# Softmax sums of an attention stage: one add chain on VectorE, or two chains on VectorE and GpSimd

## The chip, the cores and the metric

The kernel runs on one core of a Trainium2 chip, in one launch. The metric is the time on the device in microseconds, the median of several runs. A profile of one execution shows when each instruction ran on each engine: PE is TensorE (PEld its weight loads), DVE is VectorE, ACT is ScalarE, POOL is GpSimd, SP is the engine that issues most transfers.

## The reference

The network has four layers over an input of two images with 128 channels and 56 x 56 points. Each layer adds something to its input: attention, a 3x3 convolution, a mixture of experts on 2x2 patches, and a pair of Mamba scans. Only the attention layer matters here. Cut to its core:

```python
qkv = jnp.einsum('oc,bchw->bohw', w_qkv, x).reshape(B, 3, heads, hd, N)   # 4 heads of 32, N = 3136
agent = x.reshape(B, C, a, H // a, a, W // a).mean(axis=(3, 5))           # 49 averages of x
q_to_agent = softmax(einsum('bhnd,bhad->bhna', q * scale, agent))
q_compressed = einsum('bhna,bhad->bhnd', q_to_agent, agent)
attn = softmax(einsum('bhnd,bhmd->bhnm', q_compressed * scale, k))
out = einsum('bhnm,bhmd->bhnd', attn, v)
out = einsum('bnc,oc->bno', out, w_proj) + b_proj
out = layer_norm(out)
```

The large part is `attn` and `out`: for every one of 3136 queries, 3136 exponentials in each head, their weighted average of the values, and their sum, by which the average is divided.

## The kernel before

The layer is the function `short_attention` (L384 on). It works without subtracting a maximum in the softmax. Queries go in blocks of 448 (`BLK`), 7 to an image, 14 in all. Keys go in tiles of 128, 25 to an image, the last of 64. One block is a loop over 25 steps (`STEPS`), a tile of keys each.

A step `i` of a block does this. `score(i)` (L573): TensorE multiplies the tile's keys with the block's queries, head by head, into a PSUM tile `sc`; ScalarE takes the exponential (L586) into `ex`, an SBUF tile of 128 x 4 x 448 fp32, of which there are five in turn. VectorE then adds `ex` to a running sum `ex_sum` (L590 the first of a group, L592 the others). `average` (L594), one step later, multiplies the values with `ex` on TensorE and gathers the product in the PSUM tile `av` over the 25 steps. When it is complete ScalarE copies it to `att`.

The sums that the softmax divides by are still spread over the 128 partitions of `ex_sum`, one per key in a tile. `sum_up` (L615) adds them over partitions with a product of ones: `full`, a matrix of ones, times `ex_sum`, for the four heads, into the PSUM tile `den`. In the kernel before, five tiles make one group (`SUM = 5`), so a block has five `ex_sum` and five products, four in its own loop and the last at step 2 of the next block.

The rest of a block's work is spread over the steps of the next block by a table, `after`: `divide` (L628: `rec` is the reciprocal of `den`, `att` is multiplied by it, and two reductions keep its extremes), `project` (L636: TensorE multiplies `att` with the output weights, ScalarE copies the result to `y`), `measure` (L645: bias and statistics on VectorE), `normalize` (L654: the root by a logarithm and an exponential on ScalarE, with VectorE before and after; then the scaling of `y`), `turn_back` (L667: transposes on TensorE, gain and bias on ScalarE into `z`, and `x + z` on GpSimd, L676) and `restat` (statistics for the next layer). A second table, `ahead`, spreads the preparation of the following block's queries: `q_scores`, `q_softmax` (L543: sums and reciprocal on VectorE, and the multiplication of `a_e` on GpSimd, L548), `q_turn`, `q_mix`. What an image needs at its start (normalization, keys, values) is in a list `rest`, of which a step takes one item where it has no other stage; the second image's items run in the first two blocks.

The order on TensorE, ScalarE and VectorE is written out by hand: each engine takes its instructions in the order in which the loop emits them. A stage that reads a PSUM tile returns a function, `fetch`, which is called at the start of the next step. So an instruction that waits holds up all that is behind it on its engine. Within a step, the add of `score` comes ahead of the stage from `after` or `ahead`. In the attention layer GpSimd has only L548 and L676 once in each block, apart from a few fills.

Of the kernel before, what the change touches and what calls it, by code (L numbers as in the profile page):

```python
# [8 lines left out]
F32 = mybir.dt.float32  # L9
# [8 lines left out]
P = 128  # L18
# [3 lines left out]
BLK = 448  # L22
# [361 lines left out]
def short_attention(net, wide, conv):  # L384
# [12 lines left out]
    tc, nc, a = net.tc, net.nc, net.a  # L397
    heads, hd, agents, side = 4, 32, 49, 7
# [1 line left out]
    na = heads * agents  # L400
    tiles = [(m, min(P, N - m)) for m in range(0, N, P)]
    STEPS = len(tiles)
    SUM = 5
    with ExitStack() as ctx:
        one = ctx.enter_context(tc.tile_pool(name="l0_one", bufs=1))
        work = ctx.enter_context(tc.tile_pool(name="l0_work", bufs=2))
        ps = ctx.enter_context(tc.tile_pool(name="l0_ps", bufs=3, space=PSUM))
# [26 lines left out]
        full = one.tile([P, P], F32, name="full")  # L434
# [88 lines left out]
        class Block:  # L523
# [49 lines left out]
            def score(self, i):  # L573
                at, size = tiles[i]
                if i == 0:
                    self.ex, self.total = {}, {}
                ex = work.tile([P, heads, BLK], F32, name="ex", tag="ex", bufs=5)
                self.ex[i] = ex
                for g in range(2):
                    sc = ps.tile([P, 2, 512], F32, name="sc", tag="sc")  # L580
                    for j in range(2):
                        rows = slice((2 * g + j) * hd, (2 * g + j + 1) * hd)
                        nc.tensor.matmul(  # L583
                            sc[:size, j, :BLK], self.m.k[rows, at : at + size], self.q[rows, :], start=True, stop=True
                        )
                    nc.scalar.activation(ex[:size, 2 * g : 2 * g + 2, :], sc[:size, :, :BLK], AF.Exp, scale=scale)  # L586
                g, n = divmod(i, SUM)
                if n == 1:
                    self.total[g] = work.tile([P, heads, BLK], F32, name="ex_sum", tag="ex_sum")
                    nc.vector.tensor_add(self.total[g], self.ex[i - 1], ex)  # L590
                elif n > 1:
                    nc.vector.tensor_add(self.total[g][:size], self.total[g][:size], ex[:size])  # L592

            def average(self, i):  # L594
                at, size = tiles[i]
# [16 lines left out]

                    return fetch

            def sum_up(self, g):  # L615
                if g == 0:
                    self.den = ps.tile([P, 512], F32, name="den", tag="den", bufs=1)
                for h in range(heads):
                    rows = slice(h * hd, (h + 1) * hd)
                    nc.tensor.matmul(  # L620
                        self.den[rows, :BLK],
                        full[:, rows],
                        self.total[g][:, h, :],
                        start=g == 0,
                        stop=g == STEPS // SUM - 1,
                    )

            def divide(self):  # L628
                rec = work.tile([P, BLK], F32, name="rec", tag="rec")
                nc.vector.reciprocal(rec, self.den[:, :BLK])  # L630
                nc.vector.tensor_mul(self.att, self.att, rec)
                nc.vector.tensor_reduce(ends[:, 0, self.m.b, self.k : self.k + 1], rec, AX.X, ALU.max)
                nc.vector.tensor_reduce(ends[:, 1, self.m.b, self.k : self.k + 1], rec, AX.X, ALU.min)
# [33 lines left out]
            def turn_back(self):  # L667
                z_ps = bank("z_ps")
                for t in range(NT):
                    nc.tensor.transpose(z_ps[:, t * T : (t + 1) * T], self.y[:, t, :], net.ident[:T, :T])  # L670

                def fetch():
                    z = work.tile([P, BLK], F32, name="z", tag="z")
                    nc.scalar.activation(z, z_ps[:, :BLK], AF.Identity, bias=ln_b, scale=ln_g)
                    x = net.xb(self.m.b, self.k)
                    nc.gpsimd.tensor_add(x, x, z)  # L676

                return fetch
# [26 lines left out]
        def values_of(m):  # L705
# [2 lines left out]

        after = {
            4: "divide",  # L710
            6: "project",
            8: "measure",
            10: "normalize",
            13: "turn_back",
            16: "restat",
        }
        ahead = {9: "q_scores", 11: "q_softmax", 15: "q_turn", 18: "q_mix"}
        rest = values_of(images[0])[5:] + taps + opening(images[1])
# [1 line left out]
        with tc.manual_schedule(engines={E.PE, E.Activation, E.DVE}):  # L720
            nc.scalar.preload_act_table_set(EXP_LN)
            late = None
            for stage in opening(images[0]):
                fetch = stage()
                if late:
                    late()
                late = fetch
            late()
            fetches, waiting = [], []
            prev = None  # L730
            for n, blk in enumerate(blocks):
                if n == len(blocks) - 2:
                    pad = one.tile([P, PAD * PAD], F32, name="pad0", tag="xn0")
                    rest = [lambda: conv.norm(0, banks, "mm")]
                    rest += [lambda k=k: conv.pad(0, pad, k) for k in range(NBLK)]
                for i in range(STEPS):
                    for f in fetches:
                        f()
                    fetches = []
                    blk.score(i)  # L740
                    waiting.append((blk, i))
                    quota = 0 if i == 1 else 2 if i == 3 else 1
                    if n == 0 and i == 0:
                        quota = 0
                    for _ in range(quota):
                        if len(waiting) > 1:
                            who, at = waiting.pop(0)
                            fetches.append(who.average(at))
                    if i == 2 and prev:
                        prev.sum_up(STEPS // SUM - 1)  # L750
                    if i >= SUM + 2 and (i - 2) % SUM == 0:
                        blk.sum_up((i - 2) // SUM - 1)
                    stage = None
                    if i in after and prev:
                        stage = getattr(prev, after[i])
                    elif i in ahead and n + 1 < len(blocks):
                        stage = getattr(blocks[n + 1], ahead[i])
                    elif rest and (i > 2 or n == 0):
                        stage = rest.pop(0)
                    if stage:  # L760
                        fetches.append(stage())
                    fetches = [f for f in fetches if f]
                prev = blk
            assert not rest
            while waiting:
                who, at = waiting.pop(0)
                fetches.append(who.average(at))
            prev.sum_up(STEPS // SUM - 1)
            for f in fetches:
                if f:  # L770
                    f()
            tail = [getattr(prev, after[i]) for i in sorted(after)]
            tail[4:4] = [None]
            for k in range(NBLK):
                if k < len(tail) and tail[k]:
                    fetch = tail[k]()
                conv.block(0, k, pad, bank("conv_ps"))
                if k < len(tail) and tail[k] and fetch:
                    fetch()


            bad = net.small.tile([P, 4], F32, name="bad", tag="bad")
            nc.vector.memset(bad, 0.0)
            worst = net.small.tile([P, 4], F32, name="worst", tag="worst")
            aflat = asum.rearrange("t b k h -> t (b k h)")
            for n, (v, op, cmp, limit) in enumerate(
                (
                    (ends[:, 0].rearrange("p b k -> p (b k)"), ALU.max, ALU.is_gt, 1e20),
                    (ends[:, 1].rearrange("p b k -> p (b k)"), ALU.min, ALU.is_lt, 1e-30),
                    (aflat, ALU.max, ALU.is_gt, 1e30),  # L790
                    (aflat, ALU.min, ALU.is_lt, 1e-20),
                )
            ):
                size = v.shape[0]
                nc.vector.tensor_reduce(worst[:size, n : n + 1], v, AX.X, op)
                nc.vector.tensor_single_scalar(bad[:size, n : n + 1], worst[:size, n : n + 1], limit, cmp)
            total = net.small.tile([P, 1], F32, name="bad_sum", tag="bad_sum")
            nc.vector.tensor_reduce(total, bad, AX.X, ALU.add)
            w_ps = bank("w_ps")
            nc.tensor.matmul(w_ps[0:1, 0:1], full[:, 0:1], total, start=True, stop=True)  # L800
            nc.vector.tensor_single_scalar(wide, w_ps[0:1, 0:1], 0.5, ALU.is_gt)
# [1121 lines left out]
```

## Time and profile before

The time before is 3321.07 us (median of 3 runs, 3318.82 to 3325.81). The profiled execution has a span of 3329.8 us.

| | PE | DVE | ACT | POOL |
|---|---|---|---|---|
| busy, whole span | 2938.9 us (88%) | 2182.6 us (66%) | 1699.1 us (51%) | 1466.8 us (44%) |
| busy from 40 to 953 us (attention) | 861.1 us | 723.6 us | 665.1 us | 74.4 us |

The span begins with the loads and the first image's preparation. The attention blocks run from about 40 to 953 us, then come convolution, experts and the Mamba layer. GpSimd's busy time in the first row is nearly all in the Mamba layer.

A line for a group of instructions in the profile gives source line, engine, operation, the tiles written and read with their shapes, and the count; then the time in which the group kept its engine busy and the mean of one in ns; then the time its engine stood idle just before them, and whom it waited for. A line of windows gives a stretch, its length, the busy time of each engine with the number of instructions, and at the end the clock granted to TensorE as a share of full speed, the share of time in which the transfers were busy, and GB/s. A line of waits gives who waited for whom: total us, number of times, longest. A matrix product in fp32 shows as two instructions.

### The profile page before, as it was taken

The page shows a single profiled execution, that of the slowest core. Times are in us where ns is not written, and L with a number is a line of the kernel's source. Part 1 is how long each engine was busy: PE and PEld are TensorE (multiplying, and loading weights), DVE is VectorE, ACT ScalarE, POOL GpSimd, SP SyncE. Part 2 cuts the span into 40 slices and gives each one's busy share as a digit, 9 for nine tenths or more (in the row PEclk, how much of TensorE's full clock was granted, in tenths as well). Part 3 has the DMA queues.
Part 4 walks back from the last instruction along what each step waited for, and adds up shares of the span by engine and source line. Part 5 has one row for each costly group of instructions (what it writes and reads, how often), then busy time and mean ns, then how long its engine had stood idle before and what let it go on. Part 6 is the DMA issues. An engine that isn't in the chain of part 4 may idle for free. (4 is left out here: it accounts for less than half of the span.)

```text
span 3329.8 us, 34063 instructions
## 1 busy us (share of the span) xinstructions
PE 2938.9 (88%) x12828; PEld 1137.2 (34%) x12828; DVE 2182.6 (66%) x1893; ACT 1699.1 (51%) x2504; POOL 1466.8 (44%) x854
## 2 busy tenths in 40 slices
PE   6999999999999799999986788888888888888885
PEld 3333333333334444444443222333323333233321
DVE  5777887887864211111113588888988889888896
ACT  5677777777630111111101466666666665666653
POOL 2000010010000000000003689989999888898896
PEclk9999999999998799999997788988888888888986
DMA  1000000000001687787753544343543435434350
GB/s 50 1 1 1 1 1 1 1 1 1 1 18 37 242 325 291 292 321 300 289 226 109 104 97 88 64 96 79 107 84 71 93 73 107 85 70 93 74 105 7
DMA packets 133396, 333.61 MB, mean 100 GB/s; under 512 B 20101, under 2 KB 90597, under 8 KB 129621
## 3 DMA queue, kind: packets, MB, share of 16 engines
q1 hardware_dynamic: 111616, 304.87, 32.0%
q0 software_dynamic: 5136, 14.70, 1.3%
q10 hardware_dynamic: 16452, 11.61, 1.1%
q8 instruction: 104, 1.70, 0.2%
q14 instruction: 88, 0.71, 0.1%
HBM read 262.56 MB, written 17.20 MB: 84 GB/s over the span
## 5 line engine op out<-in xcount | busy, mean ns | idle before, releaser
L1658 POOL TENSOR_TENSOR dBu<-dtu,Bs 128x896 f32<-128x896 f32 x448 | 947.6, 2139 | 80.0 <-DVE h L1680 66.2
L1680 DVE TENSOR_TENSOR_SCAN h<-dA,dBu 128x896 f32<-128x896 f32 x448 | 887.8, 2010 | 144.1 <-ACT dA L1647 83.7
L586 ACT ACTIVATE ex<-sc 128x896 f32<-128x896 f32 (+1 forms) x700 | 601.4, 918 | 148.0 <-PE sc L583 134.9
L1700 PE MATMUL y<-h,both 128*64 128x448 f32 x1792 | 482.7, 638 | 44.9 <-POOL h L1686 42.3
L592 DVE TENSOR_TENSOR ex_sum<-ex_sum,ex 128x1792 f32<-128x1792 f32 (+1 forms) x210 | 446.1, 2124 | 93.7 <-ACT ex L586 85.1
L583 PE MATMUL sc<-q,k 32*128 32x448 f32 (+1 forms) x2800 | 417.4, 597 | 4.7 <-ACT ex L586 4.1
L1197 PE MATMUL h_ps<-w,xs_c 128*128 128x512 f32 x896 | 392.1, 595 | 10.4 <-issue 9.9
L1647 ACT ACTIVATE dA<-dt,f_A 128x448 f32<-128x448 f32 x448 | 284.2, 636 | 193.2 <-DVE h L1680 163.4
L548 POOL TENSOR_TENSOR a_e<-a_e,a_inv 112x784 f32<-112x784 f32 x14 | 41.6, 2974 | 728.8 <-DVE a_inv L547 728.8
L600 PE MATMUL av<-ex,va 128*32 128x448 f32 (+1 forms) x2800 | 339.5, 560 | 0.0
L1689 DVE TENSOR_TENSOR h<-h,c_ps 128x1792 f32<-128x1792 f32 x154 | 311.3, 2021 | 42.9 <-PE c_ps L1666 28.6
L1647 ACT ACTIVATE dA<-dt,b_A 128x448 f32<-128x448 f32 x448 | 281.5, 635 | 77.9 <-DVE h L1680 69.7
L1201 DVE TENSOR_TENSOR he<-h_ps,sg 128x512 f32<-128x512 f32 x56 | 38.6, 691 | 396.8 <-PE h_ps L1197 373.7
L1148 POOL DMA_INDIRECT xr<-xd,whom x28 | 28.0, 1000 | 600.0 <-PE xr_ps L1187 488.8
L1666 PE MATMUL c_ps<-low,sel_c 40*128 40x448 f32 x308 | 188.2, 696 | 114.9 <-DVE h L1689 73.7
L1686 POOL TENSOR_TENSOR h<-h,Cs 128x1792 f32<-128x1792 f32 x70 | 279.1, 3987 | 19.4 <-issue 18.4
L1197 PEld LDWEIGHTS h_ps<-w,xs_c 128*128 128x128 f32 x896 | 168.5, 190 | 218.4 <-issue 201.9
L1700 PEld LDWEIGHTS y<-h,both 128*64 128x64 f32 x1792 | 121.2, 153 | 356.3 <-issue 273.2
L583 PEld LDWEIGHTS sc<-q,k 32*128 32x128 f32 (+1 forms) x2800 | 142.0, 183 | 239.6 <-issue 128.0
L1218 PE MATMUL o_ps<-w,ht 128*128 128x512 f32 x448 | 200.2, 600 | 7.7 <-DMA w<-in_L_conv_w_dram 7.7
L590 DVE TENSOR_TENSOR ex_sum<-ex 128x1792 f32<-128x1792 f32 x70 | 141.5, 2022 | 89.0 <-ACT ex L586 88.9
L1220 ACT ACTIVATE ot<-o_ps,share 128x512 f32<-128x512 f32 x28 | 19.3, 688 | 286.9 <-PE o_ps L1218 286.9
(322 smaller groups left out, 2972.6 us busy)
## 6 DMA issues: line engine op xcount, KB each, us to landing
w<-in_L_conv_w_dram SPq DMA_DIRECT2D x28, 4096.0 KB, 19.3
w<-in_L_conv_w_dram SPq DMA_DIRECT2D x28, 2048.0 KB, 10.1
Bs<-far SPq DMA_DIRECT2D x56, 896.0 KB, 10.5
dtu<-sp_u SPq DMA_DIRECT2D x112, 224.0 KB, 3.7
dt<-dt SPq DMA_DIRECT2D x112, 224.0 KB, 5.2
Cs<-far SPq DMA_DIRECT2D x140, 112.0 KB, 7.4
os<-ot ACTq DMA_DIRECT2D x28, 256.0 KB, 7.5
xd<-xt SPq DMA_DIRECT2D x14, 224.0 KB, 2.7
```

The lines of the kernel that those rows point to most:

```text
L583: nc.tensor.matmul(sc[:size, j, :BLK], self.m.k[rows, at : at + size], self.q[rows, :], start=True, stop=True)
L586: nc.scalar.activation(ex[:size, 2 * g : 2 * g + 2, :], sc[:size, :, :BLK], AF.Exp, scale=scale)
L592: nc.vector.tensor_add(self.total[g][:size], self.total[g][:size], ex[:size])
L600: nc.tensor.matmul(self.av[rows, :BLK], self.m.va[:size, i, rows], self.ex[i][:size, h, :], start=i == 0, stop=i == STEPS - 1,)
L1197: nc.tensor.matmul(h_ps, xc[:, q, :], w1[:, q, f0 : f0 + 512], start=q == 0, stop=q == 3)
L1218: nc.tensor.matmul(o_ps, ht[:, i, :], w2[:, i, :], start=i == 0, stop=i == nj - 1)
L1647: nc.scalar.activation(self.dA[u][:, r * BLK : (r + 1) * BLK], self.dt2[:, m, r, :], AF.Exp, scale=self.w.A[:, j, 2 * m + r : 2 * m + r + 1],)
L1658: nc.gpsimd.tensor_tensor(self.dBu[u], self.dtu2[:, m], self.B[:, j, :].unsqueeze(1).to_broadcast(shape), ALU.mult)
L1680: nc.vector.tensor_tensor_scan(hf, af, bf, 0.0, ALU.mult, ALU.add)
L1686: nc.gpsimd.tensor_tensor(h4, h4, c, ALU.mult)
L1689: nc.vector.tensor_tensor(h4, h4, c, ALU.mult)
L1700: nc.tensor.matmul(self.y[r * H : (r + 1) * H, m, :BLK], both, self.hc[j][:, m, r, :], start=False, stop=j == PAIRS - 1)
```

## The change

The adding of exponentials is split. Eight of the 25 tiles of a block (`FAR`) are added up by GpSimd in a tile `ex_far`, by seven adds; VectorE adds up the other 17 in one `ex_sum`. After its add of step 19 (`JOIN`) VectorE adds `ex_far` to its sum. A block then needs one product of ones, at step 2 of the next block, where there were five. The change is meant to take the four other products from TensorE and part of the adding from VectorE, and to give `att` more time to be ready: `project` is at step 7 where it was at 6, and the stages after it move along. Two small tiles, `rec` and `z`, have one buffer where they had two, which makes room for `ex_far`.

```diff
-    SUM = 5
+    FAR, JOIN = (0, 1, 3, 5, 7, 9, 13, 15), 19
...
-                g, n = divmod(i, SUM)
-                if n == 1:
-                    self.total[g] = work.tile([P, heads, BLK], F32, name="ex_sum", tag="ex_sum")
-                    nc.vector.tensor_add(self.total[g], self.ex[i - 1], ex)
-                elif n > 1:
-                    nc.vector.tensor_add(self.total[g][:size], self.total[g][:size], ex[:size])
+                if i in FAR:
+                    if i == FAR[1]:
+                        self.far = work.tile([P, heads, BLK], F32, name="ex_far", tag="ex_far", bufs=1)
+                        nc.gpsimd.tensor_add(self.far, self.ex[FAR[0]], ex)
+                    elif i != FAR[0]:
+                        nc.gpsimd.tensor_add(self.far, self.far, ex)
+                else:
+                    near = [n for n in range(i) if n not in FAR]
+                    if len(near) == 1:
+                        self.total = work.tile([P, heads, BLK], F32, name="ex_sum", tag="ex_sum")
+                        nc.vector.tensor_add(self.total, self.ex[near[0]], ex)
+                    elif near:
+                        nc.vector.tensor_add(self.total[:size], self.total[:size], ex[:size])
+                if i == JOIN:
+                    nc.vector.tensor_add(self.total, self.total, self.far)
...
-            def sum_up(self, g):
-                if g == 0:
-                    self.den = ps.tile([P, 512], F32, name="den", tag="den", bufs=1)
+            def sum_up(self):
+                self.den = ps.tile([P, 512], F32, name="den", tag="den", bufs=1)
                 for h in range(heads):
                     rows = slice(h * hd, (h + 1) * hd)
                     nc.tensor.matmul(
-                        self.den[rows, :BLK],
-                        full[:, rows],
-                        self.total[g][:, h, :],
-                        start=g == 0,
-                        stop=g == STEPS // SUM - 1,
+                        self.den[rows, :BLK], full[:, rows], self.total[:, h, :], start=True, stop=True
                     )
...
-                rec = work.tile([P, BLK], F32, name="rec", tag="rec")
+                rec = work.tile([P, BLK], F32, name="rec", tag="rec", bufs=1)
...
-                    z = work.tile([P, BLK], F32, name="z", tag="z")
+                    z = work.tile([P, BLK], F32, name="z", tag="z", bufs=1)
...
             4: "divide",
-            6: "project",
-            8: "measure",
-            10: "normalize",
-            13: "turn_back",
-            16: "restat",
+            7: "project",
+            10: "measure",
+            12: "normalize",
+            14: "turn_back",
+            17: "restat",
...
                     if i == 2 and prev:
-                        prev.sum_up(STEPS // SUM - 1)
-                    if i >= SUM + 2 and (i - 2) % SUM == 0:
-                        blk.sum_up((i - 2) // SUM - 1)
+                        prev.sum_up()
```

## The prediction

> **What bounds the kernel now.** I read the sums of the attention stage first, then its groups of instructions, then the waits, then the order in time of a few microseconds. The stage runs from 40 to 953 us.
>
> ```profile
> 40.00:953.00 913.00, 861.09 (x6659) 285.92 (x6655) 723.57 (x640) 665.10 (x829) 74.35 (x42) 0.97 0.00 1
> L583 PE MATMUL sc<-q,k 32*128 32x448 f32 (+1 forms) x2796 | 417.0, 597 | 4.1 <-ACT ex L586 4.1
> L600 PE MATMUL av<-ex,va 128*32 128x448 f32 (+1 forms) x2800 | 339.5, 560 | 0.0
> L620 PE MATMUL den<-ex_sum,full 128*32 128x448 f32 x552 | 66.4, 554 | 0.0
> L592 DVE TENSOR_TENSOR ex_sum<-ex_sum,ex 128x1792 f32<-128x1792 f32 x196 | 417.9, 2132 | 91.6 <-ACT ex L586 84.3 <-DVE ex_sum L590 0.5
> L590 DVE TENSOR_TENSOR ex_sum<-ex 128x1792 f32<-128x1792 f32 x70 | 141.5, 2022 | 89.0 <-ACT ex L586 88.9
> ...
> PE y_ps L639 <- DVE att L631: 32.0, 13, 2.7
> ACT ir_t L69 <- DVE ir_v L68: 19.2, 15, 6.9
> ```
>
> The first line is the stage by engine in the order PE, PEld, DVE, ACT, POOL: TensorE is busy 861 of 913 us, VectorE 724, ScalarE 665, GpSimd 74. TensorE sets the pace. VectorE's two groups of sums stand idle some 180 us in all, nearly always for ScalarE's exponentials, so VectorE follows with slack. The largest idle time of TensorE is the projection, 32.0 us, for `att`. The copies `att<-av` (L611) start between 119.1 and 953.5 us, 14 of them, so a block takes 834.4 / 13 = 64.2 us. The first block, with the second image's preparation in it, takes about 80.
>
> ```profile
> 339.00:341.00 2.00, 2.00 (x13) 0.50 0.00 0
> 343.00:345.00 2.00, 2.00 (x21) 0.94 0.00 0
> 345.00:347.00 2.00, 2.00 (x20) 1.00 0.00 0
> ```
>
> After the projection's wait (TensorE idle until 337.1 us) the granted clock, the third figure from the right, is 0.50 until about 343 us. So that gap of 2.7 us costs another 3 us of slow products.
>
> The lines that decide my forecast are about GpSimd and VectorE together:
>
> ```profile
> L548 POOL TENSOR_TENSOR a_e<-a_e,a_inv x14: 1501/3087/3090, 33.3 to 862.8; 112x784 f32<-112x784 f32 x14
> L676 POOL TENSOR_TENSOR x<-x,z x14: 1132/2916/2925, 157.2 to 992.0; 128x448 f32<-128x448 f32 x14
> L1686 POOL TENSOR_TENSOR h<-h,Cs x70: 3963/3986/4008, 1873.4 to 3286.0; 128x1792 f32<-128x1792 f32 x70
> ...
> 357.72 3.09 POOL L548 TENSOR_TENSOR a_e<-a_e,a_inv 112x784 f32<-112x784 f32 x1 [59.03 <-DVE a_inv L547]
> 360.77 2.92 POOL L676 TENSOR_TENSOR x<-x,z 128x448 f32<-128x448 f32 x1
> ...
> 357.50 1.96 DVE L592 TENSOR_TENSOR ex_sum<-ex_sum,ex 128x1792 f32<-128x1792 f32 x1
> 359.56 3.13 DVE L592 TENSOR_TENSOR ex_sum<-ex_sum,ex 128x1792 f32<-128x1792 f32 x1
> 362.79 2.78 DVE L592 TENSOR_TENSOR ex_sum<-ex_sum,ex 128x1792 f32<-128x1792 f32 x1
> ```
>
> The first three give shortest, middle and longest duration in ns; the rest are single instructions, start and duration in us. L548 takes 1.50 us once and 3.09 mostly. Put the five in order: VectorE's add ends at 359.46; L548, issued at 357.72, ends at 360.81, 1.35 us after that; VectorE's second add, issued at 359.56, ends at 362.69, 1.88 after L548; L676 ends at 363.69, 1.00 later; the third add ends at 365.57, 1.88 later. They run strictly one after the other, in turn, and the wait is inside the recorded duration.
>
> **What the Trainium skill says.** "SBUF — State Buffer", Who interferes with whom: a VectorE instruction with two SBUF inputs and a GpSimd instruction that reads SBUF exclude each other, for the whole instruction. The five lines above agree to a tenth of a microsecond. In the last layer VectorE's scan takes one input from PSUM, so L1686 there is uncontended: 3.96 to 4.01 us. "GPSIMD Engine Reference", 3.1, gives 4497 ns for an fp32 add of 2048 columns, about twice VectorE's; L1686's 3987 for 1792 columns fits it. "TensorE: Matmul & The Clock Gate", Part 1: an idle TensorE falls to half clock and needs about 3.4 us of work to come back; the trace shows 0.50, after a gap that is even shorter.
>
> **The change, part by part.**
>
> *Products of ones.* Each block had 5 groups of 8 `den` instructions, now one. That removes 56 of 70 groups: 66.4 us x 56/70 = 53 us of TensorE, 3.8 a block. TensorE falls to 808 us, 58 a block. This counts only while TensorE is the bound.
>
> *Projection at step 7, the later stages moved after it.* Removes up to 2.5 us of waiting and 3 us of half clock a block, again only if `att` then is in time.
>
> *VectorE's adds.* It had 20 a block. Now 17 of the 25 tiles are its own: 16 adds and the join, 17. At 2.1 us that is 6 us of VectorE less.
>
> *GpSimd's adds.* Seven of 128x1792. No such add is in the trace; L1686 is the nearest, 3.99 us (multiply in place, one operand repeated), and L676, an add without repeated operand, gives the same rate: 1.13 us for 448 columns and 3.99 for 1792 make 2.13 ns a column. Lower end 3.7, upper 4.3; I take 3.99. Without the 0.14 us that L548 and L676 spend outside the exclusion (1.50 against 1.35, 1.13 against 1.00) one holds VectorE's two-input adds off for 3.85 us.
>
> *The shared read.* GpSimd: 7 x 3.85 + 1.35 (L548) + 1.00 (L676) = 29.3 us a block. VectorE: 17 adds x 1.9 = 32.3, plus `att*rec` 0.55, `y+b_proj` 0.68 and the small ones 0.3 = 33.8. Together 63.1 us a block that can't overlap, beside 64.2 now. So the two engines that were to share the work become one resource, full even if no gap is ever left.
>
> *Gaps in it.* Both engines take their instructions in order. From one block's last add to the next one's, where the waits fall (GpSimd in program order):
> - head: far 1, far 3, add 4, far 5 (the reciprocal, 2.95, lies beside it), `att*rec`, far 7 (the two reductions beside it), add 6, add 8, far 9, add 10;
> - middle: measure 0.68 + 0.87 + 0.36 = 1.9, add 11, softmax of the next queries 0.96 + 0.25 = 1.2, add 12, root 1.2 (352.10 to 353.3 us in a block of before), the exponentials of step 13, 1.75 (scaling and `a_e` beside them), far 13, add 14, far 15, add 16;
> - tail: `x+z` 1.0, add 17, statistics 0.6, adds 18, 19, join, 20 to 24.
>
> The exponentials are in this chain because ScalarE's logarithm for the root is queued ahead of step 13's: ScalarE waits for VectorE's `ir_v`, and all exponentials, then TensorE's scores, wait behind it. Seven far adds make 27.0; six adds taken in turn with GpSimd (4, 6, 10, 14, 16, 17) 6 x 1.9 = 11.4; eleven back to back at 2.1 (2.02 and the gap of 0.1 seen at 359.46 to 359.56) 23.1; the rest 0.55 + 1.9 + 1.2 + 1.2 + 1.75 + 1.0 + 0.6 = 8.2. Sum 69.7 us. This assumes that VectorE never runs dry and nothing else slips past; I take 69.0. Five `ex` buffers let the sums lag about four steps, so TensorE doesn't feel each wait, only the sum of them.
>
> So 69.0 - 64.2 = 4.8 us over 13 blocks = 62 us more. The first block has no stages of a previous one but the second image's preparation on VectorE; I add 3. Forecast 3321 + 65 = 3386 us. The gain on TensorE, 3.8 us of products and up to 5.5 of the projection a block, is spent waiting.
>
> **Rivals.**
> - *Packed (faster).* GpSimd's adds fall where VectorE waits for exponentials or does one-input work. Then the 63.1 us bind: 1.1 x 13 = 14 us less, 3307. For it: the far tiles alternate with near ones, so the turns are regular. Against: GpSimd stands behind `a_e`, which waits for VectorE's softmax, while VectorE has ten adds on end with GpSimd empty. A few of the gaps kept give no change, 3315 to 3328.
> - *TensorE stays the bound (faster).* Were the adds independent: 64.2 - 3.8 - 5.5 = 55, some 57 with remaining waits: 7 x 13 = 94 less, 3227. Against: the five lines.
> - *The lag feeds itself (slower).* ScalarE's wait for the root leaves TensorE idle for some 5 us or more, and then at half clock; the project, normalize and turn-back stages find late inputs too. 73 us a block: 8.8 x 13 + 10 = 124 more, 3445. For it: 0.50 after each gap now. Against: slow TensorE steps lie beside adds that are still queued.
>
> **How the numbers follow.** The chain near 69 us: 0.55. Packed 0.17, with 0.04 more for TensorE as the bound; no change 0.05; feeding itself 0.19. Faster 0.21, same 0.05, slower 0.74. The range goes from the packed case, 3300, to the self-feeding one, 3450; what is left out is the free TensorE and the far ends of both.
>
> **What would show it.** Far adds of 128x1792 that last up to 6 us, the far turn and a waiting near add in it; VectorE's `ex_sum` adds over 2.7 us in the mean, where 2.13 was; VectorE over 90% busy by the record in these slices, TensorE's share down to 85% or less; `ir_t` waiting for `ir_v` far longer than 19 us; `den` down to some 13 us. The copies of `att` would be 69 us apart. I am wrong if the adds on both engines keep 2.0 and 4.0 us at once, or if the copies come under 64 us apart.

## The result and the profile after

The changed kernel takes 3455.13 us in the median (4 runs, 3451.74 to 3457.32) beside 3323.44 us before: 132 us more, a ratio of 1.0392 with a 95% interval of 1.0368 to 1.0416. The direction was as forecast, the size was twice the forecast 65 us, and the time lies 5 us above the range.

The last copy `att<-av`, near the end of the attention stage, started at 953.5 us and now starts at 1079.6. These are the stage's sums from 40 to 1085 us (PE, PEld, DVE, ACT, POOL, granted clock), its largest groups, and its waits.

```profile
40.00:1085.00 1045.00, 876.51 (x6205) 287.14 (x6204) 774.36 (x598) 667.75 (x830) 501.77 (x140) 0.89 0.00 1
...
L584 PE MATMUL sc<-q,k 32*128 32x448 f32 (+1 forms) x2792 | 446.7, 630 | 88.9 <-ACT ex L587 88.9
L644 PE MATMUL y_ps<-wpt,att 128*112 128x128 f32 x104 | 21.7, 375 | 30.9 <-DVE att L636 30.9
L629 PE MATMUL den<-ex_sum,full 128*32 128x448 f32 x104 | 13.2, 580 | 10.4 <-DVE ex_sum L600 10.4
...
L593 POOL TENSOR_TENSOR ex_far<-ex_far,ex 128x1792 f32<-128x1792 f32 x84 | 358.3, 4265 | 135.4 <-ACT ex L587 133.2
L591 POOL TENSOR_TENSOR ex_far<-ex 128x1792 f32<-128x1792 f32 x14 | 70.4, 5026 | 296.0 <-ACT ex L587 276.1 <-DVE ex_sum L600 20.0
...
L600 DVE TENSOR_TENSOR ex_sum<-ex_sum,ex 128x1792 f32<-128x1792 f32 x196 | 496.5, 2533 | 148.3 <-ACT ex L587 139.2 <-DVE ex_sum L600 0.5
...
ACT ir_t L69 <- DVE ir_v L68: 115.0, 15, 13.2
```

`den` is down from 66.4 to 13.2 us, and TensorE is nevertheless busy for longer than before (876 against 861 us): the clock is 0.89 where it was 0.97, and `sc` takes 630 ns instead of 597. TensorE is idle for 169 of these 1045 us, more than half of it before `sc`, which waits for ScalarE (88.9 us, 4.1 before). ScalarE waits 115 us for the root's input from VectorE (19.2 before). VectorE and GpSimd each wait for exponentials too, but seldom at the same time, as will be seen. ScalarE hardly ever waits for an `ex` buffer that GpSimd still reads: 0.2 us in all by the profile's waits, so a late release of buffers by the slower engine is not what costs here.

Two single instructions show the exclusion; columns are start, duration, engine.

```profile
507.57 4.00 POOL L593 TENSOR_TENSOR ex_far<-ex_far,ex 128x1792 f32<-128x1792 f32 x1
...
510.00 3.45 DVE L598 TENSOR_TENSOR ex_sum<-ex 128x1792 f32<-128x1792 f32 x1 [6.38 <-ACT ex L587]
```

GpSimd's add ends at 511.57. VectorE's add, begun at 510.00, ends at 513.45, 1.88 us after it: the same 1.88 as in the kernel before. And this is TensorE across the wait for the root, then the clock (third figure from the right) over it:

```profile
533.92 0.96 PE L610 MATMUL av<-ex,va 128*32 128x448 f32 x8
534.81 1.02 PE L584 MATMUL sc<-q,k 32*128 32x448 f32 x4
541.90 1.86 PE L584 MATMUL sc<-q,k 32*128 32x448 f32 x4 [6.07 <-ACT ex L587]
543.70 1.72 PE L610 MATMUL av<-ex,va 128*32 128x448 f32 x8
...
525.00:533.00 8.00, 8.00 (x68) 3.18 (x62) 3.79 (x3) 6.71 (x9) 4.00 (x1) 1.00 0.01 2
541.00:545.00 4.00, 3.10 (x12) 0.71 (x12) 1.84 (x8) 3.38 (x5) 2.20 (x1) 0.50 0.01 2
```

After 6 us without work the eight `av` products take 1.72 us; just before it, at full clock, they took 0.96.

From the starts of the copies `att<-av` I took the time of a plain block (five in the middle, the fifth copy to the tenth), and from the records the time in which VectorE or GpSimd had a tensor-tensor instruction running (the two together, overlap counted once):

| | block, us | VectorE or GpSimd at a tensor-tensor instruction | difference |
|---|---|---|---|
| before | 62.4 | 43.8 | 18.6 |
| after | 71.7 | 64.7 | 7.0 |

The difference isn't idle time, since VectorE does other work in it. In the changed kernel VectorE or GpSimd has an instruction of some kind running in 68.7 of the 71.7 us; both stand idle together for 3.0.

### The profile page after: what moved, and what is told of

It is laid out like the page before. It is cut to its first block, busy times and chain, and to the rows that moved or that the text cites. A ratio compares the mean times of both kernels' runs of the same rounds, so it can differ in the third digit from the quotient of the medians.

```text
span 3452.7 us, 33289 instructions
## 1 busy us (share of the span) xinstructions
PE 2953.5 (86%) x12380; PEld 1139.5 (33%) x12380; DVE 2232.4 (65%) x1851; ACT 1701.2 (49%) x2504; POOL 1894.2 (55%) x952
## 5 line engine op out<-in xcount | busy, mean ns | idle before, releaser
L1661 POOL TENSOR_TENSOR dBu<-dtu,Bs 128x896 f32<-128x896 f32 x448 | 947.1, 2138 | 76.2 <-DVE h L1683 62.4
L600 DVE TENSOR_TENSOR ex_sum<-ex_sum,ex 128x1792 f32<-128x1792 f32 (+1 forms) x210 | 528.5, 2517 | 150.4 <-ACT ex L587 140.0
L584 PE MATMUL sc<-q,k 32*128 32x448 f32 (+1 forms) x2800 | 447.8, 630 | 89.5 <-ACT ex L587 88.9
L593 POOL TENSOR_TENSOR ex_far<-ex_far,ex 128x1792 f32<-128x1792 f32 x84 | 358.3, 4265 | 135.4 <-ACT ex L587 133.2
L610 PE MATMUL av<-ex,va 128*32 128x448 f32 (+1 forms) x2800 | 353.9, 581 | 0.1
L584 PEld LDWEIGHTS sc<-q,k 32*128 32x128 f32 (+1 forms) x2800 | 151.5, 196 | 336.1 <-issue 167.8
L591 POOL TENSOR_TENSOR ex_far<-ex 128x1792 f32<-128x1792 f32 x14 | 70.4, 5026 | 296.0 <-ACT ex L587 276.1
L1223 ACT ACTIVATE ot<-o_ps,share 128x512 f32<-128x512 f32 x28 | 19.2, 687 | 285.8 <-PE o_ps L1221 285.8
```

The lines of the kernel that those rows point to most:

```text
L584: nc.tensor.matmul(sc[:size, j, :BLK], self.m.k[rows, at : at + size], self.q[rows, :], start=True, stop=True)
L593: nc.gpsimd.tensor_add(self.far, self.far, ex)
L600: nc.vector.tensor_add(self.total[:size], self.total[:size], ex[:size])
L610: nc.tensor.matmul(self.av[rows, :BLK], self.m.va[:size, i, rows], self.ex[i][:size, h, :], start=i == 0, stop=i == STEPS - 1,)
L1661: nc.gpsimd.tensor_tensor(self.dBu[u], self.dtu2[:, m], self.B[:, j, :].unsqueeze(1).to_broadcast(shape), ALU.mult)
```

## The experiments

Fifteen kernels, each timed in three rounds beside the kernel before. "Block" is a plain block as above. A far add is one of GpSimd's, of the tiles in `FAR`. Where several lines of a table of steps change, the cuts of code below join them in one line.

| run | ratio to before (95% interval) | median, us | block, us |
|---|---|---|---|
| changed kernel | 1.0392 (1.0368 to 1.0416) | 3455.1 | 71.7 |
| e1_all_vector | 1.0208 (1.0177 to 1.0239) | 3394.7 | 68.2 |
| e2_table_only | 1.0077 (1.0052 to 1.0103) | 3352.8 | 64.9 |
| e3_no_far | 1.0098 (1.0065 to 1.0131) | 3361.7 | 65.9 |
| e4_far_fills | 1.0121 (1.0091 to 1.0151) | 3366.5 | 65.9 |
| f1_after_spread | 1.0416 (1.0395 to 1.0437) | 3459.6 | 72.6 |
| f2_before_spread | 1.0070 (1.0042 to 1.0097) | 3342.2 | 64.9 |
| f3_no_far_spread | 1.0005 (0.9998 to 1.0013) | 3323.3 | 63.7 |
| f4_three_far_spread | 1.0278 (1.0259 to 1.0298) | 3414.8 | 69.9 |
| g1_before_split | 0.9825 (0.9808 to 0.9841) | 3269.2 | 59.0 |
| g2_after_split | 1.0477 (1.0455 to 1.0499) | 3487.2 | 74.4 |
| g3_no_far_split | 0.9814 (0.9797 to 0.9830) | 3265.5 | 58.3 |
| g4_three_groups_split | 0.9876 (0.9857 to 0.9895) | 3281.8 | 59.0 |
| h1_after_late | 1.0261 (1.0241 to 1.0282) | 3413.3 | 68.2 |
| h2_three_far_late | 1.0185 (1.0163 to 1.0206) | 3386.6 | 66.4 |
| h3_all_vector_late | 0.9969 (0.9953 to 0.9985) | 3315.6 | 61.8 |

### First: which part of the change costs

All adds by VectorE, one product:

```diff
-    FAR, JOIN = (0, 1, 3, 5, 7, 9, 13, 15), 19
+    FAR, JOIN = (), None
```

> The changed kernel without its GpSimd part: VectorE adds all 25 tiles into one sum (24 adds a block), one product of ones, projection at step 7. Theory (shared SBUF read): nothing on GpSimd excludes VectorE any more but L548 and L676, so a block costs VectorE's own work, 24 x 2.1 + 11.5 = 62 us, near the 62.1 to 63.7 us of the kernel before; 3290 to 3335 us. Rival (the late sum or the new table is what costs): one sum a block is still only complete after step 24, so it stays above 3400 us.

The table of steps alone, in the kernel before (`SUM = 5` kept):

```diff
-            6: "project",  8: "measure",  10: "normalize",  13: "turn_back",  16: "restat",
+            7: "project",  10: "measure",  12: "normalize",  14: "turn_back",  17: "restat",
```

> The kernel before with nothing but the new table of steps (project 7, measure 10, normalize 12, turn_back 14, restat 17). Theory: the table is harmless and takes away most of the wait for att and the half clock after it, 2 to 5 us a block, 3255 to 3300 us. Rival (the table is what costs, since later stages fall on VectorE's and ScalarE's fuller steps): 3340 us or more.

Far adds left out:

```diff
-                    if i == FAR[1]:
-                        self.far = work.tile([P, heads, BLK], F32, name="ex_far", tag="ex_far", bufs=1)
-                        nc.gpsimd.tensor_add(self.far, self.ex[FAR[0]], ex)
-                    elif i != FAR[0]:
-                        nc.gpsimd.tensor_add(self.far, self.far, ex)
+                    pass
...
-                if i == JOIN:
-                    nc.vector.tensor_add(self.total, self.total, self.far)
```

> The changed kernel with GpSimd's seven adds and the join left out: the exponentials of eight tiles are missing from the sums. VectorE has 16 adds a block, TensorE one product of ones. Theory: TensorE is the bound again at 57 to 59 us a block, 3230 to 3275 us. Rival (the one product at step 2 and the table hold TensorE up): above 3330 us.

Far adds that write and hardly read:

```diff
-                        nc.gpsimd.tensor_add(self.far, self.ex[FAR[0]], ex)
+                        nc.gpsimd.tensor_add(self.far[:, 0, :8], self.ex[FAR[0]][:, 0, :8], ex[:, 0, :8])
                     elif i != FAR[0]:
-                        nc.gpsimd.tensor_add(self.far, self.far, ex)
+                        nc.gpsimd.tensor_add(self.far[:, 0, :8], self.far[:, 0, :8], ex[:, 0, :8])
+                    if i != FAR[0]:
+                        nc.gpsimd.memset(self.far, 0.0)
+                        nc.gpsimd.memset(self.far, 0.0)
```

> The changed kernel with each GpSimd add of 128x1792 replaced by an add of 128x8, which keeps its wait for the exponentials, and two fills of 128x1792 after it, which only write: GpSimd is as long at it (about 3.9 us by the fills of the page, 1.03 ns a column) but reads almost nothing. The far exponentials are then missing from the sums. Theory (VectorE and GpSimd exclude each other over reads): VectorE's adds go back to 2.03 us in the mean and the time falls to within 15 us of the run without far adds, 3230 to 3290 us. Rival (what costs is GpSimd's length itself, by its queue, the join that waits for it, and L548 behind it): 3400 to 3455 us.

The fills settle what it is in the far adds that costs. They came within 5 us of the run without far adds, though not in the range expected for either, with GpSimd busy 429 of 960 us in the stage, against 502 of 1045 in the changed kernel:

```profile
L596 POOL MEMSET ex_far<- 128x1792 f32 x98 | 157.4, 1606 | 5.6
L595 POOL MEMSET ex_far<- 128x1792 f32 x98 | 156.3, 1595 | 5.8
...
L603 DVE TENSOR_TENSOR ex_sum<-ex_sum,ex 128x1792 f32<-128x1792 f32 x196 | 395.5, 2018 | 181.5 <-ACT ex L587 174.9 <-DVE ex_sum L603 0.5
```

VectorE's adds are back at 2018 ns (2533 in the changed kernel). A join that waits for GpSimd, and GpSimd's length (a small add of 0.46 us and two fills of 1.60 where an add took some 4.0), cost nothing to speak of; GpSimd's reads cost 3455 - 3366 = 89 us, measured against a kernel in which nobody adds these tiles. Against e1, in which VectorE adds them, the far adds cost 3455 - 3395 = 60 us. So about half of the 132 us is there without any far add.

e3 and e4 are themselves 1% slower than before, e1 2.1%, and the table alone is already 0.8% slower. e1, e2 and e3 came out 50 to 90 us above what my theory expected, and the rivals named for e2 and e3 held; e1 lies between its two. The waits say why, here two of e2 and, last, one of e1 (up to 1000 us):

```profile
ACT ir_t L69 <- DVE ir_v L68: 69.8, 15, 6.8
...
PE sc L583 <- ACT ex L586: 42.5, 26, 3.1
...
ACT ir_t L69 <- DVE ir_v L68: 120.3, 15, 8.9
```

In e2 the projection's wait of 32 us is gone, and in its place ScalarE waits 70 us for the root. In e1, without a far add, it waits at least as long for it as in the changed kernel. In the new table the statistics, the softmax of the next queries and the root stand at steps 10, 11 and 12, the root behind an add in VectorE's queue. With the kernel before's groups of five, step 10 has no add, and there the root was.

### Second: moving the root

```diff
-            12: "normalize",  14: "turn_back",  17: "restat",
+            13: "normalize",  16: "turn_back",  19: "restat",
```

The changed kernel with this table:

> The changed kernel, all adds as they are, but with the root for the normalization at step 13 where it was 12, turn_back at 16 (14) and restat at 19 (17). Theory (the table makes ScalarE wait: measure, the softmax of the next queries and the root stand on end in VectorE's queue at steps 10 to 12, and exponentials stand behind the root on ScalarE): ScalarE's wait for ir_v falls from 115 us to under 30 and a block from 71.7 us to 66 to 68, as the shared read still holds the adds; 3380 to 3420 us. Rival (the shared read alone sets the block, and the root's wait is only where it shows): no change, 3440 to 3460 us.

The kernel before with it:

> The kernel before with the table 7, 10, 13, 16, 19 in place of 6, 8, 10, 13, 16, and nothing else. Theory: att is in time at step 7 and the root doesn't hold ScalarE, so TensorE neither idles nor falls to half clock; 4 to 6 us less a block, 3250 to 3290 us. Rival (the product groups and their waits hold TensorE anyway, or the stall only moves): 3315 us or more.

Without far adds:

> The run without far adds (the exponentials of eight tiles are missing from the sums) with the table 7, 10, 13, 16, 19. Theory: the root's wait cost TensorE 5.5 us of idle time and some 3 us of half clock a block, so a block goes from 65.6 to 57 to 58 us; 3235 to 3265 us. Rival (half clock and idle time are hidden by something else): 3330 us or more.

And with `FAR, JOIN = (0, 1, 3, 5), 19`:

> The changed kernel with the table 7, 10, 13, 16, 19 and three GpSimd adds (tiles 0, 1, 3 and 5 far) in place of seven; VectorE has 21 adds a block with the join. Theory (each far add takes 3.85 us from the shared read and gives back an add of 1.9): the shared read is taken for 3 x 3.85 + 2.35 + 21 x 1.9 + 1.5 = 55 us, VectorE's own work is 21 x 2.1 + 11.5 = 56 us, TensorE's 57; a block takes 59 to 63 us, 3270 to 3330 us, and beats the version with seven by 70 us or more. Rival (fewer far adds leave VectorE too much): slower than the version with seven under the same table.

The theory fell for the changed kernel (3459.6, just in the rival's range) and for the kernel before (3342.2, the rival's). Without far adds (3323.3) the time lies between the two: the step's delay gave 2.2 us a block there (65.9 to 63.7), not the eight expected. A step's delay isn't enough, because VectorE's lag isn't over at step 13: in f2 it works from 464.65 to 494.2 us with two gaps of 0.31 and 0.51, through the reciprocal, the statistics, the softmax, the root and nine adds. ScalarE's wait is still 61.4 us there and 64.3 in f3; in f1 it is 123.7 us up to 960 us alone, more than the 115 of the whole stage that it was to remove. With three far adds in place of seven the gain was 45 us, not 70, and the time lies 85 us above its range.

### Third: the root taken apart

Here VectorE prepares the root's input with the statistics, and ScalarE's part comes six steps later, when VectorE has caught up:

```diff
             def measure(self):
...
+                nc.vector.tensor_scalar_add(self.ve, self.mv[:, :, 1], 1e-5)
             def normalize(self):
-                net.inverse_root(rstd, self.mv[:, :, 1])
+                nc.scalar.activation(tt, self.ve, AF.Ln)
+                nc.scalar.activation(rstd, tt, AF.Exp, scale=-0.5)
...
+            7: "project",  10: "measure",  16: "normalize",  19: "turn_back",  22: "restat",
```

In the kernel before:

> The kernel before, but the root is taken apart: VectorE adds the small constant to the variance right after its statistics at step 10, and ScalarE's logarithm and exponential, VectorE's rest and the scaling come at step 16; project at 7, turn_back 19, restat 22. Theory (VectorE lags from step 4 to 13, since the reciprocal, the statistics and the softmax of the next queries lie there on top of its adds; any ScalarE instruction that waits for it in that stretch stops the exponentials, then TensorE, which comes back at half clock): ScalarE's wait for the root goes under 5 us in all, a block takes 58 to 61 us, 3265 to 3305 us. Rival (the lag stops the exponentials anyway, by the five ex buffers): 3320 us or more.

In the changed kernel:

> The changed kernel with the root taken apart in the same way. Theory: the shared read (63 us a block that can't overlap) is left as the bound and ScalarE's stop is gone: 65 to 69 us a block, 3370 to 3425 us. Rival (the adds' lag reaches the exponentials by the ex buffers instead, so that nothing is won): 3440 us or more.

Without far adds:

> The run without far adds (eight tiles' exponentials are missing from the sums), with the root taken apart in the same way. Theory: TensorE alone is left, 56.5 to 58.5 us a block, 3230 to 3265 us, which is what the one product of ones and the later projection are worth where nothing stops the exponentials. Rival: another wait takes over, above 3300 us.

The fourth kernel is the one before with `SUM = 9`, the last group shorter:

> The kernel before with three groups of nine, nine and seven tiles in place of five of five (22 adds of VectorE and three products of ones a block), no GpSimd adds, and the root taken apart in the same way. Theory: TensorE is asked for 2 products less, VectorE for 22 x 2.1 + 11.5 = 58 us: about 58 to 60 us a block, 3255 to 3300 us, faster than before. Rival (VectorE's fuller queue stops the exponentials by the ex buffers): 3320 us or more.

In the kernel before the theory held: 59.0 us a block and 1.75% less time (interval 1.6 to 1.9%), a version that beats both. The first line below is all that ScalarE waits for the blocks' roots, the second its stage from 439 to 911 us:

```profile
ACT ir_t L659 <- DVE ve L654: 9.5, 1, 9.5
...
439.00:911.00 472.00, 465.60 (x3693) 152.77 (x3690) 407.08 (x366) 365.25 (x453) 39.63 (x15) 0.99 0.00 1
```

It waits once, where it waited 13 times and more. TensorE is busy 465.6 of 472 us at a clock of 0.99. g3 tells what the four products are worth in that state: 59.0 against 58.3 us a block with nothing for GpSimd to add, 0.7 us, although 3.8 us of products (and four of VectorE's adds) are gone. g4 gave no more either: 59.0 us a block, and 13 us more than g1 in all.

With all far adds (g2) the same edit made it slower, 74.4 us a block. Nothing stops ScalarE at the root now, so the adds are still late at the block's end, and TensorE meets them at step 2, at the one product:

```profile
PE den L629 <- DVE ex_sum L600: 62.7, 9, 7.0
```

TensorE waits up to 7.0 us for the last add; then there are no exponentials, and both adders run dry. The brackets of these two single instructions give how long GpSimd and VectorE had stood, together from 510.32 to 515.81 us:

```profile
515.81 3.99 POOL L593 TENSOR_TENSOR ex_far<-ex_far,ex 128x1792 f32<-128x1792 f32 x1 [9.49 <-ACT ex L587]
...
519.70 2.03 DVE L598 TENSOR_TENSOR ex_sum<-ex 128x1792 f32<-128x1792 f32 x1 [9.38 <-ACT ex L587]
```

### Fourth: nothing in a queue that meets the sums

The root stays apart; the cut shows the other steps against g2.

```diff
-                    if i == 2 and prev:
+                    if i == 5 and prev:
                         prev.sum_up()
...
-            4: "divide",  7: "project",  10: "measure",  16: "normalize",  19: "turn_back",  22: "restat",
+            7: "divide",  10: "project",  12: "measure",  17: "normalize",  20: "turn_back",  23: "restat",
```

All seven far adds:

> The changed kernel with all its adds, but with the product of ones at step 5 (2), divide at 7 (4), project at 10 (7), measure at 12, the root taken apart as in the runs before (its ScalarE part at 17), turn_back at 20 and restat at 23, so that neither TensorE's nor ScalarE's queue meets the sums before they have caught up. Theory (in the changed kernel the shared read is taken for 64.7 of 71.7 us a block, and the 7 us between are the times when a waiting product, projection or root has stopped the exponentials and both adders run dry): the gaps close and the shared read alone sets the block, 64.5 to 67 us, 3370 to 3410 us, still slower than before. Rival (the two adders' order leaves the gaps by itself, GpSimd waiting behind the multiplication of a_e and VectorE adding alone at the end): 70 us or more a block, 3430 us or more.

With `FAR, JOIN = (0, 1, 3, 5), 19`:

> The same late table with three GpSimd adds in place of seven, VectorE with 21 adds a block. Theory: the shared read is asked for about 4 x (3.85 - 1.95) = 7.6 us less, 57 us, VectorE's own work is 56 us and the two can't overlap fully; 59 to 63 us a block, 3275 to 3335 us, 60 to 110 us below the version with seven. Rival (the number of far adds doesn't matter, the one late product does): within 20 us of the version with seven.

With `FAR, JOIN = (), None`:

> The same late table with no GpSimd add: VectorE adds all 25 tiles into one sum, 24 adds a block. Theory: VectorE's own work of 24 x 2.1 + 11.5 = 62 us is the bound, 61 to 63 us a block, 3300 to 3330 us: no better than before, since it gives TensorE's gain to VectorE, but better than seven far adds. Rival (GpSimd's help pays where nothing waits): slower than the version with seven far adds.

h1 came out between its two theories: 68.2 us a block. The adders still need 64.2 us of it, and the difference went from 7.0 to 4.0. So 3.5 of the 9.3 us by which the changed kernel's block is longer were a matter of where the waiting instructions stood. Of the 4.0 us, both engines stand idle in 1.2; in the rest VectorE does other work. The waits of h1 (up to 940 us) show one that the changed kernel doesn't have:

```profile
ACT ex L587 <- DVE ex_sum L600: 48.8, 27, 4.0
```

Here an exponential waits for an add of VectorE's, which still has to read the `ex` buffer that it will write. With nothing else in the way, the adds' lag at the block's end reaches ScalarE through the five buffers; h2 has 46.2 us of it. h2 missed: four far adds fewer gave 1.8 us a block and 27 us in all. The two adders' time fell as expected (57.1 us), but with 21 adds VectorE is at work or waiting for the exclusion 59.8 of 66.4 us, in order, so its own queue is nearly the bound there. h3, without GpSimd adds, is as expected at 61.8 us a block: 0.3% faster than before and 98 us faster than seven far adds under the same table. Along seven, three and no far adds the time goes 3413, 3387, 3316: GpSimd's help is a loss at every dose tried.

Two causes can now be held apart. Without far adds, the changed kernel's table, with the product at step 2 and the root in one piece, costs 79 us against the late one (e1 and h3, 3394.7 and 3315.6). With the late table, seven far adds cost 98 us (h1 and h3). The changed kernel has both and takes 140 us more than h3, not 177, so the two overlap in part.

## Where the prediction was right and where it failed

**The exclusion: right.** 63.1 us a block were forecast for what can't overlap; 64.7 are in the trace. Far adds last 4.27 us in the mean, some of it waiting; the forecast's `den` of some 13 us is 13.2. The fills (e4), which take the reads away and leave GpSimd's time, show the cause. The two statements of "SBUF — State Buffer", Who interferes with whom, that the forecast and this run rest on, that two-input instructions of VectorE contend with GpSimd instructions that read and not with those that only write, both agree: 2533 and 2018 ns.

**The block: 69.0 forecast, 71.7 measured. Here the first step failed.** One block can be followed from the end of its predecessor's last add, 503.62 us, to that of its own, 575.31. The order is the forecast's, but for `x+z`, which comes ahead of far 15; and the first 22.0 us, from far 1 to add 8, are 21.9 by its terms. These lines show the two places where it comes apart:

```profile
518.75 6.86 DVE L600 TENSOR_TENSOR ex_sum<-ex_sum,ex 128x1792 f32<-128x1792 f32 x2
526.58 4.00 POOL L593 TENSOR_TENSOR ex_far<-ex_far,ex 128x1792 f32<-128x1792 f32 x1 [4.98 <-ACT ex L587]
529.82 2.63 DVE L600 TENSOR_TENSOR ex_sum<-ex_sum,ex 128x1792 f32<-128x1792 f32 x1 [4.21 <-ACT ex L587]
...
537.46 3.08 POOL L549 TENSOR_TENSOR a_e<-a_e,a_inv 112x784 f32<-112x784 f32 x1 [6.89 <-DVE a_inv L548]
539.11 1.46 DVE L68 TENSOR_SCALAR ir_v<-ln_mv 112x4 f32<-112x4 f32 x1
542.80 3.98 POOL L593 TENSOR_TENSOR ex_far<-ex_far,ex 128x1792 f32<-128x1792 f32 x1 [2.26 <-ACT ex L587]
```

- Add 8 ends at 525.61 and far 9 starts at 526.58. For 0.97 us both adders wait for exponentials, which are late since the projection's wait. The forecast had nothing there: it said that TensorE "doesn't feel each wait, only the sum of them". Another 0.28 us of this kind lie ahead of far 15.
- From the end of add 12 (539.19) to far 13 it takes 3.61 us, forecast as 1.2 + 1.75 = 2.95. The forecast had `a_e` lie "beside" the exponentials. In the trace `ir_v`, 0.16 us long before, ends only with `a_e`, at 540.57, and all of ScalarE waits for it.
- The forecast's terms sum to 69.7; it took 69.0, without a reason.

These are 0.97 + 0.28 + 0.66 + 0.7 = 2.6 of the 2.7 us. The product of ones at step 2 costs the adders nothing here: GpSimd works from 502.10 to 511.57. In g2 it is what they wait for, 5.5 us together, and the block is 74.4. In h1, where the root no longer holds ScalarE in the middle, it is 68.2, 3.5 less, which fits the 3.61 us above.

The rival in which the lag feeds itself, with 73 us a block and 3445 us, had nearly the time, and its signs on TensorE came: 6.07 us idle at the root, then half clock. I gave it 0.19, with the argument that slow TensorE steps lie beside adds that are still queued. By this block it holds at the root, where far 13 starts 0.9 us after TensorE's first product at half clock. It fails after the projection: there TensorE is at half clock from 517.9 to about 524 us, and the 0.97 us follow. But both adders stand idle together for only 3.0 us of a block. So the rival was near in time, partly by luck: that slow TensorE steps set the block is not shown.

**The base: 64.2 us a block was the wrong thing to subtract, the second step that failed.** It is the mean of 13 intervals, of which the first (74.2 us) holds the second image's preparation and the twelfth (67.2) the padding for the convolution. A plain block takes 62.4. The chain of 69.0 was worked out for a plain block. Against 62.4 the two terms of a plain block are 69.0 - 62.4 = 6.6 forecast and 71.7 - 62.4 = 9.3 measured.

**Blocks with preparation: 3 us forecast for the first, 9 measured**, and the second block grew by 12.2 (74.2 to 86.4), the one with the padding by 10.8 (67.2 to 78.0). Their extra work on VectorE stands in the same queue as the adds.

By the traces the attention stage ends 126 us later, and 65 were forecast. An estimate from the figures above: 13 x 2.7 = 35 us of what is missing are the chain, 13 x 1.8 = 23 the base, 6 the first block; the other intervals together grew by 4 us less than that.

**Projection and table.** The projection waits 30.9 us (32.0 before), `att` being later by as much as the step gave. In e2, without far adds, it doesn't show among the waits. The forecast saw in the new table only a possible gain; alone it costs 0.8% (e2).

**What the gain of TensorE was worth.** The forecast let 3.8 us of products and up to 5.5 us of the projection be spent waiting, and so it is. But even in kernels without far adds the first is worth 0.7 us (g3 against g1). And the second came only when the root was moved out of VectorE's lag: g1's 3.4 us a block.

Two signs did not show. VectorE is at work or waiting inside an instruction for 53.5 us of a block of 71.7 (75%), not over 90%, since it stands idle for 18 us, 15 of them while GpSimd works. Its adds take 2.53 us in the mean, not over 2.7. And TensorE's 3.4 us of work until full clock, which the forecast quoted, are not what the traces show: in the kernel before the half clock lasts from 337.1 to about 343 us, in the changed one from 541.9 to about 548, some 6 us each.

## What to carry to other kernels

Before giving part of a VectorE chain of two-input adds to GpSimd, add up both engines' time at instructions that read SBUF as if one engine did them: a far add of 4.0 us that saves one of 2.0 was a loss here where that sum came to 57 us of a block of 66 (h2) and to 64 of 68 (h1). Then look for the small instruction in a full engine's queue that waits for the lagging one, here a logarithm on ScalarE 0.2 us long; where such an instruction stands can be worth more (in g1 57 us, 1.75%, with the later projection) than the work that one set out to remove. A mean over blocks isn't the base for a chain worked out for one: take it from plain blocks.

## What was not expected of the hardware

The root's first VectorE instruction, a `tensor_scalar` over 112x4, took 0.16 us before (13 of them, 2.1 us) and 1.36 us in the mean in the changed kernel and in e3, where it falls beside GpSimd's multiplication of `a_e`; its ScalarE reader waits for that too, as seen above. The scaling of `y`, also a `tensor_scalar`, went from 342 to 989 ns beside the fills, which only write, while two-input adds did not slow there at all. The first line is e4's, the second the changed kernel's:

```profile
L666 DVE TENSOR_SCALAR y<-y,ln_mv,ln_rstd 112x128 f32<-112x128 f32 x52 | 30.2, 989 | 0.5
L68 DVE TENSOR_SCALAR ir_v<-ln_mv 112x4 f32<-112x4 f32 x13 | 17.7, 1360 | 0.0
```

So a VectorE instruction with one SBUF tensor input can be held off as well. "SBUF — State Buffer", in the same section, says so of `tensor_scalar` where it runs in a mode with two ports, for `ir_v` as for the scaling; no trace here shows the mode. The forecast counted both as free of it.
